# A graph network's gathered blocks: one visit of six rounds in place of two of three

## The chip, the cores and the metric

The kernel runs on one core of a Trainium2 chip. The metric is the device time in microseconds of one execution; the median of the runs is quoted. The engines are named as the profile names them: PE is TensorE, DVE is VectorE, ACT is ScalarE, POOL is GpSimd, SP is the queue of SyncE. PEld is TensorE's loading of weights.

## The reference

A graph with 6250 nodes, 256 features each, and 100000 edges sorted by destination. Four layers; each adds to every node the sum of its sources' features and then runs a small dense network over the nodes.

```python
h = jnp.maximum(_layernorm(x, axis=-1), 0.0)
def agg(h):
    return jax.ops.segment_sum(h[src], dst, num_segments=N)
for l in range(NL - 1):                       # three layers, 256 -> 256 -> 256 -> 256
    h = x + agg(x)
    h = jax.nn.relu(h @ W1s[l] + b1s[l])
    h = jax.nn.relu(h @ W2s[l] + b2s[l])
    x = h @ W3s[l] + b3s[l]
h = x + agg(x)                                # the last one, 256 -> 256 -> 64 -> 256
h = jax.nn.relu(h @ cW1 + cb1)
h = jax.nn.relu(h @ cW2 + cb2)
out = x_in + (h @ cW3 + cb3)
```

## The kernel before

The nodes are cut into 49 blocks of 128. The sum over the edges is done in two ways, side by side.

Most blocks are summed by a **product**: a matrix of edge counts, 128 destinations by all nodes, is built once as bytes (layer 0 builds it while it uses it, lines 1030 to 1093), kept in DRAM and cast to fp32r when it is used (line 1565). TensorE multiplies it with the features XY, which are held in SBUF as a high and a low half. In layer 0 the products go block by block (line 1588), in layers 1 to 3 by panels of four blocks (line 1665), with single blocks (line 1588) in between. A panel has 49 steps of four matmuls with 512 columns; a step is the unit in which the program is laid out.

The other blocks are **gathered**: 23 in layer 0, 20 in layers 1 and 2, 19 in layer 3. The edges of a gathered block are held in T = 17 tiles of 128 edges. For each tile GpSimd issues an indirect DMA (line 1382) that fetches the 128 source rows from the layer's table in DRAM into one of the buffers `rows`: 24 of them in layer 0, 25 in layers 1 to 3. TensorE then adds the rows up with one-hot matrices as the weights. Because the edges are sorted, a tile can only touch a neighbourhood of the block: the block's 128 destinations are four groups of Q = 32, and tile c + 4m serves group m in round c. There are six rounds, c = -1, 0, 1, 2, 3, 4; a round is four matmuls (three for c = -1) with 32 weight columns each, which fill the four column groups of the array, and in fp32 each matmul is two instructions of the profile. So a block has 23 matmuls, 46 instructions, that add up in one bank of PSUM, `sums`.

The six rounds are done in two **visits**, ROUNDS = ((3, 1, -1), (0, 4, 2)). A visit (`add`, line 1408) is put between two steps of the products. The first needs the 8 odd tiles, the second the 9 even ones. The one-hots of a visit come from one VectorE instruction (line 1402), which compares a row of column numbers with the table `rel`; it is issued right after the visit before, and has two buffers. After a block's second visit its own features are added (lines 1439 and 1448), two blocks at a time are transposed (line 1479), and the dense network follows for four blocks at a time (lines 1233 and 1290; in the last layer 1225 and 1245).

The order of all work is fixed while the program is written out: each engine runs its instructions in that order. A planner keeps an estimated clock, which `passed` moves on with every matmul (constants in line 1508; a visit counts as VISIT = 1.7 us). When a layer's table is complete, `begin` fixes when its first visit is due, LEAD = 21 us of this clock later, and spreads the others evenly up to TAIL = 10 us before the layer's estimated end; `pace` is the time per row. `flow` sends the row requests at the same pace, LEAD ahead, and ties each to the last matmul written so far (`after`), so that GpSimd can't issue it earlier. `meets` says whether a visit is due; eight steps before the end of a layer all visits that are left are due. Steps of the dense network wait in a queue and are taken at a visit where one falls into their window, or else at the window's end (`step`). In layer 0 the first 8 requests are sent at once, before the build of the counts starts (line 1703).

Of the kernel before, what the change touches and what calls it, by code (L numbers as in the profile page):

```python
# [8 lines left out]
F32 = mybir.dt.float32  # L9
# [387 lines left out]
def sorted_edges(  # L397
# [58 lines left out]
    CUTS = ((3, 5), (7, 9), (11, 13), (0, T))  # L456
    ROUNDS = ((3, 1, -1), (0, 4, 2))
    CH = 7
# [38 lines left out]
    idx = const.tile([P, left[NQ]], I32, name="idx")  # L497
    rel = const.tile([P, left[NQ] // T, len(ROUNDS), 3, P // Q], BF16, name="rel")
    colf = const.tile([P, P], F32, name="colf")
# [117 lines left out]
    def look(pool):  # L617
# [214 lines left out]
        for t, o in ((fd, rel), (fs, idx)):  # L832
            ps = ps_m.tile([P, W], F32, name="ps")
            for q, (_, n) in enumerate(gone):
                nc.tensor.transpose(ps[:, left[q]:left[q + 1]], t[:n * T, q, :],
                                    ident[:n * T, :n * T])
            if o is rel:
                v = ps[:, :left[NQ]].rearrange("p (b k) -> p b k", k=T)
                for i, rounds in enumerate(ROUNDS):
                    for c in rounds:  # L840
                        g = 1 if c < 0 else 0
                        nc.vector.tensor_scalar(o[:, :, i, (c - min(rounds)) // 2, g:],
                                                v[:, :, c + 4 * g:c + 13:4], -1.0, None, op0=OP.add)
            else:
                nc.vector.tensor_copy(o, ps[:, :left[NQ]])
# [118 lines left out]
    with tc.manual_schedule():  # L964
# [370 lines left out]
        class Gathered:  # L1335
            def __init__(self, l):
# [10 lines left out]
                self.n = len(self.visits)  # L1347
                self.rows, self.us = {}, []

# [16 lines left out]
            def begin(self):  # L1366
                self.first = clock[0] + LEAD
                self.end = begun[self.l] + work_of(self.l) - TAIL
                self.pace = (self.end - self.first) / (self.upto[-1] - self.upto[1])
# [27 lines left out]

            def one_hots(self, v):
                g, rounds = self.visits[v]
                shape = [P, len(rounds), P // Q, Q]  # L1400
                self.hot = work.tile(shape, F32, name="hot", bufs=2)
                nc.vector.tensor_tensor(
                    self.hot,
                    colf.rearrange("p (m q) -> p m q", q=Q)[:, None, :, :].to_broadcast(shape),
                    rel[:, self.blocks[g][3] // T, v % len(ROUNDS), :, :, None].to_broadcast(shape),
                    OP.is_equal)

            def add(self):
# [3 lines left out]
                self.sums = sums  # L1412
                if v == 0:
                    self.one_hots(0)
                end = rounds == ROUNDS[-1]
                for c in rounds:
                    for m in range(P // Q):
                        if c + 4 * m >= 0:
                            nc.tensor.matmul(  # L1419
                                self.sums[m * Q:(m + 1) * Q, :C],  # L1420
                                self.hot[:, (c - min(rounds)) // 2, m, :], self.rows[g, c + 4 * m],
                                start=(c == ROUNDS[0][0]), stop=(c == ROUNDS[-1][-1]))
                passed(VISIT)
                self.done += 1
                if self.done < self.n:
                    self.one_hots(self.done)
                if end:
# [78 lines left out]
        sums = ps_g.tile([P, W], F32, name="sums")  # L1506
        LEAD, TAIL = 21.0, 10.0
        COLS, FULL32, TURN, VISIT, BUILD, BURST = 0.457e-3, 1.68e-3, 0.4, 1.7, 0.2, 0.3
        clock = [0.0]
# [183 lines left out]
        with tc.tile_pool(name="hots", bufs=1) as hots, tc.tile_pool(  # L1693
# [8 lines left out]
            layers[0].begin()  # L1702
            layers[0].send(layers[0].upto[1])
            beside = build(hots, ats, ps_b)
# [84 lines left out]
```

## Time and profile before

| | |
|---|---|
| median of 3 runs | 2130.42 us (2127.44 to 2132.5) |
| the profiled execution | 2135.8 us, its span 2134.0 us |
| TensorE, mean granted clock | 0.988 |
| PE / PEld busy | 96% / 70% of the span |
| DVE / ACT / POOL busy | 44% / 41% / 68% |
| chain that ended last, by engine | PE 88%, DVE 5%, DMA 4%, the rest 3% |
| row requests by layer, first to last | 126.6 to 674.2, 719.2 to 1163.3, 1205.7 to 1647.6, 1686.8 to 2105.0 |

A group of the profile has the line, the engine, the operation, what is written from what, the count, the busy time in us, the mean in ns of one, and then the idle time of the engine ahead of these instructions with what ended it. Rows of the timeline have start, duration, engine, line and a count of merged instructions, and in brackets the idle time ahead and what ended it. The chain is followed back from the last instruction, at each step to what released it; "issue" is time in which an engine waited for nothing that the profile shows. The view of stretches gives each engine's busy time and its instructions (x) between two times, then the granted clock, the busy share of the DMA engines and GB/s. A view of one line or tile gives the shortest, the median and the longest duration in ns, and the first and the last start.

### The profile page before, as it was taken

The numbers are of one execution on the slowest core, as the hardware profiler recorded it, in microseconds if no ns is written. First come the engines' busy times: TensorE is split into PE (matmuls) and PEld (weight loads), VectorE is DVE, ScalarE is ACT, GpSimd is POOL, SyncE is SP. The second block draws the span as 40 slices with busy tenths as digits, with TensorE's granted clock in tenths as the row PEclk, the third lists the DMA queues.
The fourth block names the chain that finished last, engine by engine and source line by source line (L and its number), as shares of the span: only waits on it lengthen the run. The fifth ranks groups of instructions, "written<-read, shape, count | busy, mean of one in ns | idle before, by whom it ended". The sixth has DMA issues, their size and how long they took to land.

```text
span 2134.0 us, 33393 instructions
## 1 busy us (share of the span) xinstructions
PE 2057.4 (96%) x12076; PEld 1487.8 (70%) x12076; DVE 937.7 (44%) x2192; ACT 864.3 (41%) x1775; POOL 1445.4 (68%) x1470
## 2 busy tenths in 40 slices
PE   4979999999999999999999999999999999999997
PEld 3756766667667777777776777777776777777675
DVE  7877867667673422222233322222233433333332
ACT  4856655556556522323232433222333432223231
POOL 2727777777774477777776377777776277777773
PEclk9979999999999999999999999999999999999999
DMA  5524545545455655455455554555456555556553
GB/s 157 176 98 139 162 142 153 158 140 164 150 158 152 213 163 155 153 181 164 142 186 167 173 160 148 173 165 169 146 168 195 170 172 181 184 180 194 183 160 119
DMA packets 184901, 347.61 MB, mean 163 GB/s; under 512 B 32446, under 2 KB 118496, under 8 KB 184726
## 3 DMA queue, kind: packets, MB, share of 16 engines
q0 software_dynamic: 68960, 185.41, 29.7%
q1 hardware_dynamic: 113838, 158.12, 22.3%
q8 instruction: 97, 1.59, 0.3%
q10 hardware_dynamic: 1928, 1.85, 0.3%
q14 instruction: 78, 0.64, 0.1%
HBM read 287.98 MB, written 57.26 MB: 162 GB/s over the span
## 4 chain that ended last, share of the span: by engine, by line
PE 88%; DVE 5%; DMA 4%; issue 1%; ACT 1%; POOL 1%; SPq 0%; DVEq 0%; POOLq 0%; ACTq 0%
PE agg L1665 43%; PE agg L1588 16%; PE sums L1419 11%; PE ps L1233 6%; PE ps L1290 6%; PE bp L1076 4%; DMA rows<-table,idx 3%; PE ps L1479 1%; POOL rows L1382 1%; DVE junk L695 1%; PE bp L920 1%; DVE hi L1035 1%; DVE at L1086 1%; PE ps L1245 0%; DMA table<-zs 0%
## 5 line engine op out<-in xcount | busy, mean ns | idle before, releaser
L1382 POOL DMA_INDIRECT rows<-table,idx x1394 | 1387.7, 995 | 611.4 <-issue 220.6
L1665 PE MATMUL agg<-a,XY 128*128 128x512 f32 x4116 | 982.8, 395 | 1.9 <-DVE clT L1600 1.9
L1665 PEld LDWEIGHTS agg<-a,XY 128*128 128x128 f32 x4116 | 764.6, 188 | 209.5 <-issue 45.8
L1565 ACT CAST a<-at 128x512 fp32r<-128x512 uint8 (+1 forms) x542 | 326.9, 616 | 576.9 <-PE agg L1665 543.9
L1565 DVE CAST a<-at 128x512 fp32r<-128x512 uint8 x543 | 242.7, 448 | 552.8 <-PE agg L1665 469.3
L1588 PE MATMUL agg<-XY,a 128*128 128x512 f32 x1470 | 404.9, 409 | 1.3 <-DVE un L1600 0.7
L1588 PEld LDWEIGHTS agg<-XY,a 128*128 128x128 f32 x1470 | 258.9, 189 | 53.7 <-issue 8.7
L1419 PE MATMUL sums<-rows,hot 128*32 128x256 f32 x3772 | 256.0, 385 | 16.2 <-DMA rows<-table,idx 15.0
L1419 PEld LDWEIGHTS sums<-rows,hot 128*32 128x32 f32 x3772 | 112.6, 109 | 142.6 <-issue 53.6
L1549 ACT CAST a<-at 128x512 fp32r<-128x512 uint8 (+2 forms) x362 | 196.7, 574 | 6.5 <-PE agg L1588 6.5
L1084 ACT CAST at<-bp 128x392 uint8<-128x392 f32 x240 | 116.6, 487 | 203.7 <-PE bp L1076 191.0
L1086 DVE CAST at<-bp 128x392 uint8<-128x392 f32 x240 | 135.1, 563 | 138.2 <-PE bp L1076 138.2
L1448 DVE TENSOR_TENSOR u<-u,sums 128x256 f32<-128x256 f32 x82 | 34.3, 419 | 241.8 <-PE agg L1665 226.9
L1076 PE MATMUL bp<-hi,lo 128*128 128x196 bf16 x960 | 127.5, 255 | 11.0 <-DVE hi L1035 10.7
L1290 PE MATMUL ps<-w,h 128*128 128x256 f32 x588 | 133.9, 379 | 1.4 <-ACT h L1236 0.9
L1233 PE MATMUL ps<-h,w 128*128 128x512 f32 (+3 forms) x332 | 133.9, 545 | 0.6 <-DVE zz L1298 0.6
L1035 DVE TENSOR_TENSOR hi<-cols,pairs 128x784 bf16<-128x784 bf16 x240 | 134.3, 560 | 0.0
L1076 PEld LDWEIGHTS <-lo 128*128 128x128 bf16 x960 | 70.6, 99 | 81.9 <-DVE hi L1035 27.8
L1290 PEld LDWEIGHTS ps<-w,h 128*128 128x128 f32 x588 | 111.1, 190 | 18.7 <-ACT h L1236 1.8
L1483 ACT ACTIVATE h<-ps,bias 128x256 f32<-128x256 f32 (+1 forms) x116 | 47.2, 464 | 154.9 <-PE ps L1479 154.9
L1298 DVE TENSOR_TENSOR zz<-ps,w 128x512 f32<-128x512 f32 (+1 forms) x75 | 50.1, 678 | 117.0 <-PE ps L1290 117.0
L1035 DVE TENSOR_TENSOR lo<-lanes,pairs 128x512 bf16<-128x512 bf16 x240 | 100.3, 418 | 1.3 <-ACT pairs L1030 1.3
(171 smaller groups left out, 989.7 us busy)
## 6 DMA issues: line engine op xcount, KB each, us to landing
at<-mat SPq DMA_DIRECT2D x151, 448.0 KB
mat<-at SPq DMA_DIRECT2D x30, 784.0 KB
rows<-table,idx POOLq DMA_INDIRECT x1394
table<-zz SPq DMA_DIRECT2D x72, 256.0 KB
back<-table SPq DMA_DIRECT2D x99, 128.0 KB
xs<-in_x_dram SPq DMA_DIRECT2D x8, 768.0 KB
table<-zs SPq DMA_DIRECT2D x24, 256.0 KB
out_dram<-zz SPq DMA_DIRECT2D x24, 256.0 KB
```

The source lines that it names most:

```text
L1035: nc.vector.tensor_tensor(o.rearrange("p q (n t) -> p q n t", t=2), values.rearrange("p (n t) -> p n t", t=2)[:, None, :, :].to_broadcast( ...
L1076: mm = nc.tensor.matmul(bp[:, m * HW:(m + 1) * HW], lo[:, q + m, :], hi[:, q + m, :], start=True, stop=True)
L1084: nc.scalar.copy(o, v)
L1086: nc.vector.tensor_copy(o, v)
L1233: mm = nc.tensor.matmul(ps[:mp, :w], weights[l][0][:, c, i * P:i * P + mp], h1[:, c, :w], start=(c == 0), stop=(c == KC - 1))
L1290: mm = nc.tensor.matmul(o, h2[0][:, c, nodes], w3[:, c, :], start=(c == 0), stop=(c == KC - 1))
L1382: got = nc.gpsimd.indirect_dma_start(out=t, out_offset=None, in_=tables[self.l][:, :], in_offset=bass.IndirectOffsetOnAxis(ap=idx[:, o:o + ...
L1419: nc.tensor.matmul(self.sums[m * Q:(m + 1) * Q, :C], self.hot[:, (c - min(rounds)) // 2, m, :], self.rows[g, c + 4 * m], start=(c == ROUND ...
L1549: nc.scalar.copy(a[:, i * m * P:(i + 1) * m * P].rearrange("p (j d) -> p j d", j=m), counts[b][:, j:j + m, :])
L1565: cast(o, at[:, :, d:d + m * P])
L1588: mm = nc.tensor.matmul(agg, a[:, d:d + P], XY[:, j, :], start=(j == 0), stop=(j == NT - 1))
L1665: mm = nc.tensor.matmul(agg[c][:, :w], XY[:, j, o:o + P], a[:, :w], start=(j == 0 and half == 0), stop=(j == NT - 1 and half == 1))
```

## The change

All six rounds of a block are done in one visit. Its one-hots are one instruction of twice the size (768 columns of fp32) into one buffer, made four steps after the visit before, and for a layer's first block when the layer begins. A visit now needs all 17 tiles of its block. LEAD goes from 21 to 32 us and VISIT from 1.7 to 3.0 us (it counted twice per block before). Layer 0's first 8 requests stay 8, now by number. `rel` has the same size in another order.

```diff
-    ROUNDS = ((3, 1, -1), (0, 4, 2))
+    ROUNDS = ((3, 1, -1, 0, 4, 2),)
...
-    rel = const.tile([P, left[NQ] // T, len(ROUNDS), 3, P // Q], BF16, name="rel")
+    rel = const.tile([P, left[NQ] // T, len(ROUNDS), len(ROUNDS[0]), P // Q], BF16, name="rel")
...
-                        nc.vector.tensor_scalar(o[:, :, i, (c - min(rounds)) // 2, g:],
+                        nc.vector.tensor_scalar(o[:, :, i, c - min(rounds), g:],
...
-                self.rows, self.us = {}, []
+                self.rows, self.us, self.hots = {}, [], -1
...
             def begin(self):
                 self.first = clock[0] + LEAD
+                self.one_hots(0)
...
             def one_hots(self, v):
+                if self.hots >= v:
+                    return
+                self.hots = v
                 g, rounds = self.visits[v]
                 shape = [P, len(rounds), P // Q, Q]
-                self.hot = work.tile(shape, F32, name="hot", bufs=2)
+                self.hot = work.tile(shape, F32, name="hot")
...
-                if v == 0:
-                    self.one_hots(0)
+                self.one_hots(v)
...
-                                self.hot[:, (c - min(rounds)) // 2, m, :], self.rows[g, c + 4 * m],
+                                self.hot[:, c - min(rounds), m, :], self.rows[g, c + 4 * m],
...
                 if self.done < self.n:
-                    self.one_hots(self.done)
+                    later(4, lambda v=self.done: self.one_hots(v))
...
-        LEAD, TAIL = 21.0, 10.0
-        COLS, FULL32, TURN, VISIT, BUILD, BURST = 0.457e-3, 1.68e-3, 0.4, 1.7, 0.2, 0.3
+        LEAD, TAIL = 32.0, 10.0
+        COLS, FULL32, TURN, VISIT, BUILD, BURST = 0.457e-3, 1.68e-3, 0.4, 3.0, 0.2, 0.3
...
-            layers[0].send(layers[0].upto[1])
+            layers[0].send(8)
```

## The prediction

> **What bounds the kernel now.** I read the page first (busy shares, then the costliest groups), then the busy time of each engine by layer, then the GpSimd queue by layer, then the chain of work at the ends of layers.
>
> ```profile
> span 2134.0 us, 33393 instructions
> ...
> PE 2057.4 (96%) x12076; PEld 1487.8 (70%) x12076; DVE 937.7 (44%) x2192; ACT 864.3 (41%) x1775; POOL 1445.4 (68%) x1470
> ...
> L1382 POOL DMA_INDIRECT rows<-table,idx x1394 | 1387.7, 995 | 611.4 <-issue 220.6
> ```
>
> By the shares TensorE bounds everything and GpSimd (POOL) has a third of its time free. The second view, one stretch per layer from its first row request to its last, has the same TensorE story: 443.21 busy of 446, 444.00 of 444.
>
> ```profile
> core 0: us, PE busy (x) PEld busy (x) DVE busy (x) ACT busy (x) POOL busy (x), PEclk, DMA share, GB/s
> 126.00:676.00 550.00, 536.78 (x3571) 371.11 (x3572) 386.71 (x893) 326.97 (x748) 394.66 (x391) 0.98 0.50 152
> 719.00:1165.00 446.00, 443.21 (x2525) 324.18 (x2523) 132.61 (x305) 140.76 (x258) 337.66 (x340) 1.00 0.56 173
> 1205.00:1649.00 444.00, 444.00 (x2534) 325.48 (x2532) 132.31 (x297) 138.86 (x251) 334.26 (x340) 1.00 0.56 172
> 1686.00:2107.00 421.00, 414.03 (x2464) 304.19 (x2462) 136.23 (x301) 126.77 (x229) 321.07 (x323) 1.00 0.59 184
> ```
>
> But GpSimd's free time is not free. The next rows are its groups in the same four stretches; the number that matters is the idle time before the requests.
>
> ```profile
> L1382 POOL DMA_INDIRECT rows<-table,idx x391 | 394.7, 1009 | 173.6 <-issue 63.9 <-PE agg L1588 45.5 <-PE bp L1076 34.8
> ...
> L1382 POOL DMA_INDIRECT rows<-table,idx x340 | 337.7, 993 | 151.5 <-issue 56.1 <-DMA back<-table 44.1 <-PE agg L1665 39.9
> ...
> L1382 POOL DMA_INDIRECT rows<-table,idx x340 | 334.3, 983 | 150.0 <-issue 53.7 <-PE agg L1665 44.7 <-DMA w<-in_L_gnn_W2s_dram 41.4
> ...
> L1382 POOL DMA_INDIRECT rows<-table,idx x323 | 321.1, 994 | 136.3 <-issue 46.9 <-DMA clT<-in_L_gnn_cW_dram 38.2 <-PE agg L1665 37.8
> ...
> 1162.09 0.95 POOL rows L1382
> 1163.04 0.30 issue
> 1163.34 3.99 DMA rows<-table,idx
> 1167.38 1.92 PE sums L1419 x10
> ```
>
> Between two requests that follow at once lies 0.30 us. Leave out each layer's one long wait for its table (44.1, 41.4, 38.2) and count 0.30 per request: layer 1 has 151.5 - 44.1 - 340 x 0.30 = 5.4 us of true idleness on GpSimd, layer 2 has 150.0 - 41.4 - 102 = 6.6, layer 3 has 136.3 - 38.2 - 96.9 = 1.2. Only layer 0 has room: 173.6 - 117.3 = 56. So in layers 1 to 3 the row requests run back to back from the moment the table is complete to the last row, at 0.99 + 0.30 = 1.29 us each, and the layer's end waits for the last of them: the chain above goes request, 3.99 us of flight, sums. TensorE is full and the request queue is full as well. A gain on TensorE in layers 1 to 3 is capped by what the queue can still give.
>
> **The change, part by part.** (1) Two visits of three rounds become one of six. A visit works the array as 128x32 tiles between full-width products; its surroundings cost time that no round needs.
>
> ```profile
> 1061.11 3.46 PE ps L1290 x16
> 1064.56 1.43 PE sums L1419 x24
> 1065.99 4.76 PE agg L1665 x20
> 1070.76 1.43 PE sums L1419 x22
> 1072.19 11.12 PE agg L1665 x48
> 1083.31 1.43 PE sums L1419 x24
> ...
> 1201.88 21.80 PE agg L1665 x96
> ...
> 161.71 1.50 PE L1419 MATMUL sums<-rows,hot 128*32 128x256 f32 x22 [1.11 <-DVE hot L1402]
> ...
> 209.44 1.50 PE L1419 MATMUL sums<-rows,hot 128*32 128x256 f32 x22
> 210.87 0.51 PE L1076 MATMUL bp<-hi,lo 128*128 128x196 bf16 x4
> ```
>
> A pass of 256 fp32 columns takes 3.46 / 16 = 0.216 us; a round is two passes (four column groups side by side), so three rounds are 1.30, and 1.43 is spent: 0.13 over. An undisturbed product runs at 21.80 / 96 = 0.227; 48 between two visits should take 10.90 and take 11.12: 0.22 more, the way in and out of a visit. A visit's surroundings thus cost about 0.35 us, and the merge removes one per block. At 17 rows a block the requests above are 23, 20, 20 and 19 blocks. Layers 1 to 3: 59 x 0.35 = 20.7 us of TensorE time (7.0, 7.0, 6.7). In layer 0 what follows is often a build (L1076) whose slow-down I cannot read off; bounds 0.13 and 0.35, taken 0.25: 5.8 us. All layers: 26.5.
>
> (2) The first one-hot is made when the layer begins, not in the first visit: the 1.11 us wait at 161.71 goes. What is late next there is nothing, the rows then have 32 planned us.
>
> (3) What of this reaches the end. Layer 0 is bound by TensorE (56 us of idle requests): all of it counts, less the last visit. At the end of a layer the planner flushes what is left eight steps before the end, and the last row then in flight now holds up a visit of six rounds, not three. Its first four rounds need rows 0, 1, 3, ... up to 15, so they can run while row 16 flies; I charge 1 us. Layer 0: -5.8 - 1.1 + 1 = -5.9. Layer 1: TensorE offers 7.0, less about 2 because with the new lead one or two requests more (1.29 each) are still unsent at the flush; GpSimd can give at most 5.4, and never all: -3.5. Layer 2: 7.0 against 6.6: -4.5. Layer 3: GpSimd has 1.2 to give, the earlier finish only lengthens TensorE's waits for rows: 0, and +0.5 for the longer last visit.
>
> (4) One-hots: one instruction of 768 columns for two of 384, in one buffer, four steps after the visit.
>
> ```profile
> L1402 DVE TENSOR_TENSOR hot<-colf,rel x164: 537/551/607, 161.1 to 2092.2; 128x384 f32<-128x384 f32 x164
> ...
> L1439 DVE TENSOR_TENSOR u<-XY x82: 410/418/427, 174.3 to 2101.3; 128x256 f32<-128x256 f32 x82
> ...
> 2037.93 0.56 DVE L1402 TENSOR_TENSOR hot<-colf,rel 128x384 f32<-128x384 f32 x1
> 2038.40 0.42 DVE L1439 TENSOR_TENSOR u<-XY 128x256 f32<-128x256 f32 x1
> ...
> 2036.73 0.95 POOL L1382 DMA_INDIRECT rows<-table,idx  x1 [0.30 <-PE agg L1665]
> 2037.98 1.33 POOL L1382 DMA_INDIRECT rows<-table,idx  x1 [0.30 <-issue]
> ...
> L1382 POOL DMA_INDIRECT rows<-table,idx x323: 947/953/1582, 1686.8 to 2105.0; - x162
> ```
>
> From 384 and 256 columns the slope is (0.551 - 0.418) / 128 = 1.04 ns a column, so 768 take 0.551 + 0.400 = 0.95: 82 x (1.10 - 0.95) = 12 us less on VectorE, which is a third busy in layers 1 to 3, so nothing by itself. The single buffer makes the one-hot wait for the visit before. Ahead of it in VectorE's order stands the add at L1448, three steps after the visit, which waits for the same sums and a product behind them; so the one-hot finds its buffer free, and the casts behind it wait for no more than before. Its cover is the distance to the next visit, some 446 / 20 = 22 us; were it gone, each visit would wait 0.95.
>
> But the request at 2037.98 met one-hot and add: 1.33 instead of 0.95. The requests of layers 1 to 3 average 0.993, 0.983 and 0.994 where the median, in the last row, is 0.953: 13.6 + 10.2 + 13.2 = 37 us in all, in the very queue that is full. If what a request loses grows with the square of an uninterrupted VectorE run (chance to meet it, times what is left of it), two of 0.55 against one of 0.95 is 0.61 to 0.90, at worst half of 37 more: +18. Yet in every second visit one-hot and add stand together today (0.98) and will stand apart: 1.26 to 1.08, -5. Between -5 and +18 I take 0, nearest to the second count, which is what the rows show.
>
> (5) The lead. It was 21 planned us for a first visit of 8 rows, now 32 for one of 17. At a planned pace near 1.35 us (an estimate; the rows come every 446 / 340 = 1.31) that is 15.6 - 8 + 1 = 8.6 rows ahead of need, and 23.7 - 17 + 1 = 7.7 now: the same. New is that 17 + 8 = 25 fills the 25 buffers (24 in layer 0, 17 + 7). A request beyond them waits on GpSimd, with all later ones behind it, until the visit is through. The count of requests issued by the start of a visit shows how far ahead the queue runs today:
>
> ```profile
> 719.00:782.75 63.75, 49.41 (x47) 1.00 0.63 202
> 719.00:1019.76 300.76, 229.45 (x230) 1.00 0.56 173
> ```
>
> The visit at 782.75 needed row 42, that at 1019.76 row 221: 5 and 9 rows ahead. With a cap of 8 the late visits cost GpSimd a row's time, but the queue is only held where it had run ahead, and 5 rows x 1.29 = 6.5 us still cover the 3.99 us flight. I take 0; the far bound is the third rival.
>
> (6) Table `rel`, its six writes, the first 8 requests: the same work in another order, 0.
>
> Sum: -5.9 - 3.5 - 4.5 + 0.5 = -13.4 us. The profiled execution took 2135.8 us for its span of 2134.0, 0.25% above the median of 2130.42; it would become 2122.4, and the median **2117.0**. Bounds of the parts: layer 0 from -3 to -9, layers 1 and 2 from -4 to -12, layer 3 from -1 to +1: 2114 to 2124 for this case.
>
> **The rivals.** *The whole TensorE gain arrives.* If the queue is not the bound, because the requests keep their pace with TensorE and only look back to back, 26.5 + 1.1 come off: 2103. For it: TensorE 99% busy in layers 1 and 2. Against it: 1.2 us of idle requests in layer 3, and layer ends that wait for rows.
>
> *The longer one-hot slows the requests.* By (4) between 9 (the one-hots behind half of the 37 us) and 18 us come back: about 2130, no change. The Trainium skill, "SBUF — State Buffer", section "Who interferes with whom", has a tensor_tensor with both inputs in SBUF contend with GpSimd's reads, the second to come blocked for the whole of the first. The trace agrees in the 1.33 us request; by that rule alone the longer instruction is the worse.
>
> *Steps move behind the last rows.* Steps of the dense layers (3.46 us at 1061.11) prefer to run at a visit and otherwise wait for their deadline; with half the visits more of them slip. One that slips past the flush in each of layers 0 to 2 costs 3 x 3.5 = 10: 2127. Against it: the last steps of a layer are hurried anyway.
>
> *The full buffers stop the queue: slower.* Each late visit leaves GpSimd idle with 25 rows out, and the queue has only 5.4 and 6.6 us of slack to catch up. Layer 3 runs behind and never fills its buffers, so it is the 40 blocks of layers 1 and 2: from 13.4 / 40 = 0.33 us lost per block on, the gain is eaten; at half a request, 0.65 us, it is 40 x 0.65 - 13.4 = +12.6, 2143; at 0.5 us, 2137. For it: 9 rows ahead at 1019.76. Against it: a held queue was ahead, and TensorE only feels it once the lead falls under the flight.
>
> **How the numbers follow.** Forecast 0.50, whole gain 0.08, one-hot 0.12, steps 0.12, buffers 0.18. A measurement of this kernel tells about 0.2%, 4.3 us, from no change: the limits are 2126.2 and 2134.7. Faster: 0.48 of the forecast, the whole gain, 0.03 of the one-hot and 0.06 of the steps: 0.65. Slower: 0.15 of the buffers, 0.04 of the one-hot and 0.01 of the steps: 0.20. The rest, 0.15, is the same. The range leaves out the whole gain and the far end of the buffers: 2108 to 2138.
>
> **What would show it.** Right: visits of 46 matmuls in 2.7 to 2.8 us; first to last row request of layer 3 still 418 us (1686.8 to 2105.0 now), of layers 1 and 2 some 4 us shorter, layer 0 5 to 6; more TensorE waiting on rows in layer 3. Wrong: a mean request above 1.00 us (one-hot), requests that wait on the sums for more than a few us in all (buffers), a 3.5 us step between the last visit and the next layer's first request that is not there today, or layer 3 shorter by 6 us (whole gain).

## The result: slower by a quarter of a per cent

The merged kernel takes 2137.67 us, median of 9 runs (2134.25 to 2141.0); the kernel before, run beside it, 2130.74 (9 runs, 2127.44 to 2135.63). The ratio on record is 1.0025, with an interval of 1.0014 to 1.0037; the two medians are 6.9 us apart, 0.33%. The forecast was 2117.0, faster by 0.6%: the direction was wrong, and the time lies at the upper end of the range.

The profile after comes from an execution of 2136.97 us. That of the kernel before, which the prediction reads, took 2135.8 us, 5 us over its median, so a second profile of the same kernel is used for the comparison: 2130.95 us, at the median. First the page of the merged kernel:

```profile
span 2134.9 us, 33269 instructions
PE 2038.4 (95%) x12076; PEld 1499.3 (70%) x12076; DVE 930.6 (44%) x2110; ACT 859.5 (40%) x1775; POOL 1448.2 (68%) x1470
L1383 POOL DMA_INDIRECT rows<-table,idx x1394 | 1390.9, 998 | 605.3 <-issue 219.1
L1422 PE MATMUL sums<-rows,hot 128*32 128x256 f32 x3772 | 249.5, 391 | 29.7 <-DMA rows<-table,idx 29.6
L1422 PEld LDWEIGHTS sums<-rows,hot 128*32 128x32 f32 x3772 | 124.2, 111 | 147.0 <-DMA rows<-table,idx 43.5
```

The busy times and the same two rows of the visits on the page of the kernel before (its second profile):

```profile
PE 2054.6 (96%) x12076; PEld 1486.3 (70%) x12076; DVE 937.6 (44%) x2192; ACT 864.2 (41%) x1775; POOL 1445.9 (68%) x1470
L1419 PE MATMUL sums<-rows,hot 128*32 128x256 f32 x3772 | 254.4, 385 | 15.1 <-DMA rows<-table,idx 14.0
L1419 PEld LDWEIGHTS sums<-rows,hot 128*32 128x32 f32 x3772 | 112.2, 109 | 140.7 <-issue 51.9
```

TensorE is busy for less time: 2038.4 us instead of 2054.6. But it waits longer for rows: 29.6 us at the visits instead of 14.0. The requests' mean (998 ns against 996 before) has hardly moved.

Where the time went is read by layer. The next two answers give the busy time of each engine from the start of one layer's products to the start of the next layer's. The kernel before:

```profile
139.60:693.30 553.70, 545.82 (x3611) 378.80 (x3611) 375.95 (x870) 331.43 (x761) 386.47 (x383) 1.00 0.49 151
693.30:1181.60 488.30, 482.87 (x2696) 354.65 (x2697) 147.78 (x339) 158.07 (x300) 337.45 (x340) 0.99 0.53 166
1181.60:1664.60 483.00, 480.34 (x2692) 352.38 (x2691) 147.21 (x331) 154.92 (x286) 334.38 (x340) 1.00 0.53 167
1664.60:2129.20 464.60, 447.40 (x2613) 327.50 (x2611) 153.02 (x340) 138.04 (x254) 322.72 (x323) 0.99 0.56 174
```

The merged kernel:

```profile
140.80:696.80 556.00, 542.39 (x3610) 383.37 (x3610) 372.74 (x846) 329.30 (x761) 383.86 (x383) 0.99 0.50 151
696.80:1182.10 485.30, 475.85 (x2696) 357.68 (x2697) 145.73 (x319) 157.52 (x300) 339.95 (x340) 0.99 0.54 167
1182.10:1664.60 482.50, 477.40 (x2691) 356.51 (x2690) 145.17 (x312) 153.28 (x286) 335.82 (x340) 0.99 0.54 167
1664.60:2134.90 470.30, 444.68 (x2615) 328.94 (x2613) 152.32 (x321) 137.58 (x255) 322.98 (x323) 0.98 0.56 172
```

The second column is the length, the third TensorE's busy time; their difference is TensorE's idle time. The clock is the third figure from the right.

| layer | length, us | TensorE busy | TensorE idle | predicted length |
|---|---|---|---|---|
| 0 | +2.3 | -3.4 | 7.9 to 13.6 | -5.9 |
| 1 | -3.0 | -7.0 | 5.4 to 9.4 | -3.5 |
| 2 | -0.5 | -2.9 | 2.7 to 5.1 | -4.5 |
| 3 | +5.7 | -2.7 | 17.2 to 25.6 | +0.5 |

Busy time fell by 16.1 us, idle time grew by 20.6. (The first profile of the kernel before has 553.1, 489.8, 484.3 and 464.1 us for the four layers: two executions of the same kernel differ by up to 1.5 us in a layer.) The granted clock is lower too: 0.982 to 0.987 in the nine executions of the merged kernel, 0.987 to 0.991 in ten of the kernel before.

**Layer 0: a lump on VectorE.** The time that the count build's matmuls (L1076) wait for VectorE's casts (L1035) over layer 0, as total, number of times and longest; before, then merged:

```profile
PE bp L1076 <- DVE hi L1035: 3.4, 10, 0.6
```

```profile
PE bp L1076 <- DVE hi L1035: 8.7, 19, 1.7
```

Its longest piece in the timeline of the merged kernel, VectorE first, then TensorE:

```profile
321.68 0.41 DVE L1451 TENSOR_TENSOR u<-u,sums 128x256 f32<-128x256 f32 x1
322.01 0.95 DVE L1406 TENSOR_TENSOR hot<-colf,rel 128x768 f32<-128x768 f32 x1
322.88 0.42 DVE L1035 TENSOR_TENSOR lo<-lanes,pairs 128x512 bf16<-128x512 bf16 x1
323.21 0.56 DVE L1035 TENSOR_TENSOR hi<-cols,pairs 128x784 bf16<-128x784 bf16 x1
```

```profile
323.83 0.51 PE L1076 MATMUL bp<-hi,lo 128*128 128x196 bf16 x4 [1.71 <-DVE hi L1035]
```

The add of the sums (0.41 us) and the 0.95 us one-hot stand together in front of the two casts for which the next build matmuls wait 1.71 us. The add of the sums ends just ahead of the one-hot in 36 of the 82 blocks of the merged kernel, 9 in each layer.

**The ends of layers: the 16th row.** The last visits of layer 2 in TensorE's timeline, before:

```profile
1640.60 1.50 PE L1419 MATMUL sums<-rows,hot 128*32 128x256 f32 x22
...
1644.10 1.06 PE L1419 MATMUL sums<-rows,hot 128*32 128x256 f32 x14
1647.20 1.05 PE L1419 MATMUL sums<-rows,hot 128*32 128x256 f32 x10 [2.04 <-DMA rows<-table,idx]
```

The last visit of layer 1, the last two of layer 2, and the last of layer 3, merged:

```profile
1158.98 1.06 PE L1422 MATMUL sums<-rows,hot 128*32 128x256 f32 x2 [4.36 <-DMA rows<-table,idx]
1164.20 4.25 PE L1422 MATMUL sums<-rows,hot 128*32 128x256 f32 x40 [4.15 <-DMA rows<-table,idx]
...
1628.22 2.80 PE L1422 MATMUL sums<-rows,hot 128*32 128x256 f32 x46
...
1637.05 0.62 PE L1422 MATMUL sums<-rows,hot 128*32 128x256 f32 x4
1638.49 0.62 PE L1422 MATMUL sums<-rows,hot 128*32 128x256 f32 x2 [0.82 <-DMA rows<-table,idx]
1642.90 5.33 PE L1422 MATMUL sums<-rows,hot 128*32 128x256 f32 x40 [3.80 <-DMA rows<-table,idx]
...
2103.80 5.33 PE L1422 MATMUL sums<-rows,hot 128*32 128x256 f32 x40 [3.35 <-DMA rows<-table,idx]
```

A block's rows are requested in the order of their numbers. The first round (c = 3) of the merged visit uses tiles 3, 7, 11 and 15, and tile 15 is the 16th of 17 requests: 6 matmuls run, and 40 wait for the row before the last. In the kernel before, only the odd tiles stand in the first visit, and only 10 matmuls wait for the last row. And the 40 take 5.33 us, where the whole visit of 46 before it takes 2.80. Busy time and clock in short stretches around the last visit of layer 3 say why:

```profile
2095.00:2100.00 5.00, 5.00 (x29) 3.69 (x30) 1.44 (x3) 2.91 (x7) 3.78 (x5) 1.00 0.37 108
2100.00:2103.80 3.80, 0.46 (x6) 0.00 (x0) 0.00 (x0) 0.00 (x0) 2.62 (x3) 0.82 0.36 104
2103.80:2106.50 2.70, 2.70 (x28) 1.32 (x32) 0.00 (x0) 0.00 (x0) 0.00 (x0) 0.50 0.18 49
2106.50:2109.10 2.60, 2.60 (x21) 0.85 (x13) 0.00 (x0) 0.00 (x0) 0.00 (x0) 0.50 0.00 0
2109.10:2112.00 2.90, 2.28 (x10) 1.63 (x10) 1.62 (x4) 0.00 (x0) 0.00 (x0) 0.97 0.00 0
```

After the wait of 3.35 us TensorE's clock is 0.50 for the whole 5.3 us of the visit. The length of the wait alone does not decide this. Here are waits of the kernel before (first and second profile) and of the merged kernel with half of its requests (an experiment below):

```profile
1652.49 1.05 PE L1419 MATMUL sums<-rows,hot 128*32 128x256 f32 x10 [3.28 <-DMA rows<-table,idx]
...
1907.46 1.05 PE L1419 MATMUL sums<-rows,hot 128*32 128x256 f32 x10 [2.53 <-DMA rows<-table,idx]
1908.50:1911.50 3.00, 3.00 (x8) 2.42 (x8) 0.93 (x2) 0.00 (x0) 2.13 (x3) 0.50 0.35 102
...
1156.94 4.46 PE L1426 MATMUL sums<-rows,hot 128*32 128x256 f32 x40 [2.13 <-DMA rows<-table,idx]
```

The wait of 3.28 us was followed by a clock of 1.00, those of 2.53 and 2.13 by a clock of 0.50 for some 3 us; the 40 matmuls behind a wait of 2.11 us in the merged kernel took 2.78 us, full speed. The Trainium skill, "TensorE: Matmul & The Clock Gate", section "Part 1: The HAM clock gate", says that an idle window of about 3.4 us halves the clock until about as long a busy one has passed. The waits of 3.35 to 4.36 us agree with it, those of 2.13 and 2.53 us do not, and the measurement decides: here waits between 2.1 and 3.3 us went either way.

Summed in slices of 1 us as (1 - clock) x TensorE's busy time, the half clock costs 2.1, 2.0, 0.0 and 2.8 us in layers 0 to 3 before, and 2.9, 2.0, 2.8 and 4.4 merged: an estimated 5.3 us more. Added to the 16.1 us by which the busy time fell, TensorE's saving at full clock is about 21 us, where the prediction had 26.5.

### The profile page after: what moved, and what is told of

It reads as the page before. It is cut to its first block, busy times and chain, and to the rows that moved or that the text cites. A ratio compares the mean times of both kernels' runs of the same rounds, so it can differ in the third digit from the quotient of the medians.

```text
span 2134.9 us, 33269 instructions
## 1 busy us (share of the span) xinstructions
PE 2038.4 (95%) x12076; PEld 1499.3 (70%) x12076; DVE 930.6 (44%) x2110; ACT 859.5 (40%) x1775; POOL 1448.2 (68%) x1470
## 3 DMA queue, kind: packets, MB, share of 16 engines
q1 hardware_dynamic: 113838, 158.12, 22.6%
## 4 chain that ended last, share of the span: by engine, by line
PE 85%; DVE 6%; DMA 4%; ACT 2%; issue 2%; POOL 1%; SPq 0%; DVEq 0%; ACTq 0%; POOLq 0%
PE agg L1668 42%; PE agg L1591 13%; PE sums L1422 11%; PE ps L1290 6%; PE ps L1233 6%; PE bp L1076 3%; DMA rows<-table,idx 3%; DVE hi L1035 1%; DVE at L1086 1%; PE ps L1482 1%; PE bp L920 1%; DVE lo L1035 1%; POOL rows L1383 1%; PE ps L586 1%; DVE hot L1406 1%
## 5 line engine op out<-in xcount | busy, mean ns | idle before, releaser
L1422 PE MATMUL sums<-rows,hot 128*32 128x256 f32 x3772 | 249.5, 391 | 29.7 <-DMA rows<-table,idx 29.6
L1422 PEld LDWEIGHTS sums<-rows,hot 128*32 128x32 f32 x3772 | 124.2, 111 | 147.0 <-DMA rows<-table,idx 43.5
L1076 PE MATMUL bp<-hi,lo 128*128 128x196 bf16 x960 | 127.9, 256 | 17.2 <-DVE hi L1035 16.5
L1035 DVE TENSOR_TENSOR hi<-cols,pairs 128x784 bf16<-128x784 bf16 x240 | 134.3, 559 | 0.0
L1076 PEld LDWEIGHTS <-lo 128*128 128x128 bf16 x960 | 72.0, 99 | 87.0 <-DVE hi L1035 37.6
L1233 PEld LDWEIGHTS ps<-h,w 128*128 128x128 f32 (+1 forms) x332 | 60.9, 189 | 56.0 <-issue 47.1
```

The lines of the kernel that those rows point to most:

```text
L1035: nc.vector.tensor_tensor(o.rearrange("p q (n t) -> p q n t", t=2), values.rearrange("p (n t) -> p n t", t=2)[:, None, :, :].to_broadcast( ...
L1076: mm = nc.tensor.matmul(bp[:, m * HW:(m + 1) * HW], lo[:, q + m, :], hi[:, q + m, :], start=True, stop=True)
L1233: mm = nc.tensor.matmul(ps[:mp, :w], weights[l][0][:, c, i * P:i * P + mp], h1[:, c, :w], start=(c == 0), stop=(c == KC - 1))
L1422: nc.tensor.matmul(self.sums[m * Q:(m + 1) * Q, :C], self.hot[:, c - min(rounds), m, :], self.rows[g, c + 4 * m], start=(c == ROUNDS[0][0] ...
```

## The experiments

**How well the same kernel repeats.** The kernel before, unchanged; it also gave the second profile used above.

> The kernel before, unchanged, run as if it were a change: it tells how far two equal kernels come apart and gives a second profile by layer. Expected on every theory: a ratio of 1.000 within 0.2%, and a profiled execution nearer the median than the first one (2135.8 against 2130.7), row requests of layers 1 to 3 again 444, 442 and 418 us from first to last.

Measured: 2131.45 us, ratio 0.9996 (0.9981 to 1.0011), as expected.

**Half of the requests left out, before and merged.**

```diff
                     g, k = self.order[self.sent]
+                    if self.sent % T % 2:
+                        self.rows[g, k] = self.rows[self.order[self.sent - 1]]
+                        self.sent += 1
+                        continue
```

> The kernel before with 9 of a block's 17 row requests: every second tile of a block uses the rows of the tile before it, so 738 requests are left and the output is not the reference's. Theory 'the request queue caps layers 1 to 3': the queue is half empty, so TensorE's waits for rows go (about 7 us at the end of layer 1, 4 of layer 2, 12 in layer 3) and the time falls by 15 to 25 us. Rival 'the queue only looks full': within 5 us of before.

> The changed kernel with the same 738 requests. Theory 'the queue caps layers 1 to 3': with the cap gone the merged visits bring their 0.35 us a block there, so it is 17 to 21 us faster than the kernel before with half the requests, all of it in layers 1 to 3. Rival 'the merge saves nothing on TensorE, or VectorE takes it back in every layer': within 6 us of it.

Measured: before 2109.15, ratio 0.9899 (0.9868 to 0.9929); merged 2094.78, ratio 0.9823 (0.9791 to 0.9855). The visits' rows on the two pages, before and merged:

```profile
L1423 PE MATMUL sums<-rows,hot 128*32 128x256 f32 x3772 | 246.8, 383 | 1.8 <-DVE hot L1406 1.1
```

```profile
L1426 PE MATMUL sums<-rows,hot 128*32 128x256 f32 x3772 | 232.3, 383 | 3.1 <-DMA rows<-table,idx 3.1
```

So the request queue is a bound of the kernel before (22 us; by the two profiles 7.1, 2.6 and 13.3 in layers 1 to 3), as the prediction read it from GpSimd's gaps. And with rows in time, the merge is worth 14.4 us: with the full queue it costs 7. That is less than the 17 to 21 expected. By layer the merge gives +1.1, -1.9, -5.4 and -6.2 us there, while TensorE's busy time falls by 19.0. The saving on TensorE is real; a good part of what eats it depends on the rows.

**The later one-hots left out.** In the merged kernel only a layer's first block makes its one-hot (4 instead of 82); in the kernel before likewise its first visit.

```diff
 merged:
-                if self.hots >= v:
+                if self.hots >= 0:
                     return
 before:
             def one_hots(self, v):
+                if v:
+                    return
```

> The changed kernel with one one-hot for a whole layer in place of one a block, which leaves out 78 of the 82 instructions at 0.95 us; the output is not the reference's. Theory 'the long one-hot stands in front of VectorE's one-hots for the build in layer 0': layer 0 gets 6 to 8 us shorter, TensorE's wait for the build falls back from 8.7 to about 3 us. Theory 'it also holds up requests': their mean in layers 1 to 3 falls from 0.998 by 0.02 or more, 7 us a layer. Together 15 to 25 us below the changed kernel. Rival 'the one-hot has no part in it': within 4 us of the changed kernel.

> The kernel before with one one-hot for a whole layer (156 to 160 of 164 instructions of 0.55 us are left out; the output is not the reference's). Theory 'layer 0 is bound by VectorE's chain already': layer 0 falls by 3 us or more from 553.6, though TensorE's work is the same, and the gain of the changed kernel without one-hots (549.3) over this one in layer 0 is under 2 us. Theory 'layer 0 is bound by TensorE and only the long one-hot broke that': layer 0 stays at 552 to 554 here, and the changed kernel without one-hots is 4 us shorter. In layers 1 to 3 the mean request falls by 0.01 to 0.02, and the total is 8 to 15 us below before.

Measured: merged 2115.08, ratio 0.9925 (0.9901 to 0.9949); before 2126.38, ratio 0.9983 (0.9968 to 0.9999). The merged kernel gives up 22.6 us with its 78 one-hots, the kernel before 4.4 with its 160: the one-hots as merged cost 18 us more, and without them the merge would gain 11.3, near the forecast's 13.4. The 22.6 is what was expected; the 4.4 is less than the 8 to 15 expected for the kernel before. In layer 0 the build's wait for the casts is back at the old value without the one-hots (merged):

```profile
PE bp L1076 <- DVE hi L1035: 3.9, 11, 0.8
```

and layer 0 of the merged kernel lasts 549.3 instead of 556.0 us; that of the kernel before 553.3 without, 553.7 with its one-hots. Without one-hots the merge gives layer 0 -4.0, close to the -5.9 of the prediction. In layers 1 to 3 it shows in the queue. The requests of these layers in the merged kernel, with and then without its one-hots:

```profile
L1383 POOL DMA_INDIRECT rows<-table,idx x340 | 339.9, 1000 | 145.3 <-PE agg L1668 77.0 <-issue 54.5 <-DMA rows<-table,idx 4.0
...
L1383 POOL DMA_INDIRECT rows<-table,idx x340 | 335.8, 988 | 143.0 <-PE agg L1668 73.9 <-issue 56.1 <-PE ps L1290 3.7
...
L1383 POOL DMA_INDIRECT rows<-table,idx x323 | 323.0, 1000 | 137.9 <-issue 43.9 <-DMA clT<-in_L_gnn_cW_dram 39.8 <-PE agg L1668 37.2
```

```profile
L1383 POOL DMA_INDIRECT rows<-table,idx x340 | 332.9, 979 | 148.1 <-PE agg L1668 76.3 <-issue 61.5 <-PE ps L1233 3.0
...
L1383 POOL DMA_INDIRECT rows<-table,idx x340 | 331.2, 974 | 146.0 <-PE agg L1668 76.9 <-issue 59.4 <-PE ps L1290 2.4
...
L1383 POOL DMA_INDIRECT rows<-table,idx x323 | 317.0, 982 | 136.9 <-issue 46.3 <-DMA clT<-in_L_gnn_cW_dram 38.8 <-PE agg L1668 33.5
```

The requests take 7.0, 4.6 and 6.0 us less. In the kernel before, the same edit takes 5.1, 3.0 and 5.9 us off them (means of 992, 983 and 999 ns to 977, 975 and 981), so the merged one-hots cost the requests only some 4 us more. But they count for more: in the kernel before the edit shortened layers 1 and 2 by only 0.5 and 0.2 us, in the merged kernel by 4.2 and 2.9; layer 3 fell in both, by 6.2 and 7.9. TensorE is busy for 482.58 of 487.8 us and 480.33 of 482.8 in layers 1 and 2 of the kernel before without one-hots; that it is TensorE that keeps the faster requests from counting there is argued, not shown. TensorE's waits for rows in the merged kernel fell from 29.6 to 19.2 us.

**The one-hot in two halves of 384 columns,** four and eight steps after the visit, in the same buffer:

```diff
-                    later(4, lambda v=self.done: self.one_hots(v))
+                    later(4, lambda v=self.done: self.one_hots(v, 1))
+                    later(8, lambda v=self.done: self.one_hots(v))
```

> The one-hots in two instructions of 384 columns, four and eight steps after the visit, once more, because the chip of the last four runs took 11% longer for the kernel before, with long gaps on GpSimd and TensorE in which neither waited for work. Expected of a chip like the first: theory 'the length of one uninterrupted VectorE run stalls the build': layer 0 3 to 5 us shorter than in the changed kernel (556), the total 4 to 10 us below 2137. Rival 'the place of the one-hot, in the middle of the build's steps, is what costs': layer 0 as in the changed kernel or longer.

Measured: 2130.45, ratio 0.9998 (0.9985 to 1.001): level with the kernel before, and below the merge's 1.0025, some 6 us, as expected. (This run, the next one, the halves with the short window and the extra product in the kernel before fell on another chip of the same speed, where the kernel before takes 2129.83 and the merged kernel wasn't run; so the ratios are compared.) Layer 0 lasts 552.7 us, 3.3 less than merged; the requests of layers 1 to 3 average 0.990, 0.987 and 0.990 us. The length of the instruction is thus a part of its price, not all: the waits for casts in layer 0 are 6.6 us, those for rows 23.6.

**The one-hot one step after the visit instead of four,** ahead of the add of the sums:

```diff
-                    later(4, lambda v=self.done: self.one_hots(v))
+                    later(1, lambda v=self.done: self.one_hots(v))
```

> The changed kernel with the one-hot one step after the visit in place of four: the same instruction of 768 columns, placed where VectorE has to wait for the visit itself, which still reads the single buffer. Theory 'the place costs': layer 0 3 to 6 us shorter than the changed kernel's 556. Theory 'the length costs': layer 0 the same within 2 us, or longer by up to 5, since VectorE now also stands still until the visit of 2.7 us is through.

Measured: 2132.54, ratio 1.0015 (1.0005 to 1.0025). The interval overlaps the merge's (1.0014 to 1.0037), so a gain in the whole time isn't shown. No one-hot stands behind an add any more, and layer 0's wait for casts is 7.0 us with a longest of 0.8, where it was 8.7 and 1.7; but layer 0 lasts 554.2 us, 1.8 less than merged. That is within the 2 us of 'the length costs', not the 3 to 6 of 'the place costs'.

**A shorter window for the dense steps** (3 instead of 6), in both kernels, and with the halves:

```diff
-        FAR, SPAN = 7, 6
+        FAR, SPAN = 7, 3
```

> The kernel before with SPAN at 3. Theory 'SPAN repairs what the merge did to the steps': with two visits a block a step meets a visit in time anyway, so the time stays within 3 us of before, the tail after the last request near 28 us as before. Rival 'a shorter window is better for any kernel': 5 to 10 us below before, as much as on the changed kernel.

> The changed kernel with SPAN at 3 and its one-hots as they are. Theory 'the slipped steps cost the tail': from the last request to the end 28 to 30 us in place of 32.6, the total 3 to 8 us below the changed kernel, 2130 to 2135. Rival 'the gain of the combined kernel came from the split one-hots with some luck': 2136 to 2139.

> Split one-hots and SPAN at 3 together, on the changed kernel: the two losses that the trace of the changed kernel shows beside the full queue. If both theories hold (layer 0 -4, the tail after the last request from 32.6 us to about 28) the time is 7 to 12 us below the changed kernel: 2125 to 2130, at or just under the kernel before. If only the tail holds: 2132 to 2135. If neither: 2137.

Measured: before 2121.71, ratio 0.9956 (0.9943 to 0.9969); merged 2128.71, ratio 0.9988 (0.9972 to 1.0004); merged with halves 2122.28, ratio 0.9956 (0.9942 to 0.997). The window is worth 9 us to either kernel, as the rival 'a shorter window is better for any kernel' had it, so steps that slip are not what makes the merge slower: it stays 7.0 us behind with the short window, though its tail from the last request to the end fell from 32.6 to 25.9 us (before: 27.8 to 25.1). With the halves its ratio is level with that of the kernel before, as it was with the long window. The waits for rows at the visits with the window of 3, before and then merged:

```profile
PE sums L1419 <- DMA rows<-table,idx: 6.4, 6, 2.7
```

```profile
PE sums L1422 <- DMA rows<-table,idx: 22.4, 11, 4.5
```

The kernel before now waits 6.4 us in pieces of at most 2.7, the merged one 22.4 in pieces of up to 4.5. On these chips the kernel before with the window of 3 and the merged one with halves and window share the lowest ratio of those that compute the reference, 0.9956; no merged version was shown to beat the kernel before with the same window.

**One more block as a product instead of gathered** in layers 1 and 2, in the kernel before (34 requests fewer, more TensorE work):

```diff
-        solos = [[], [19], [19], [18, 19]]
+        solos = [[], [18, 19], [18, 19], [18, 19]]
-        order = [[]] + [[0, 1, 2, 19, 3, 4, 5, 6]] * 2 + [[0, 1, 18, 2, 3, 19, 4, 5, 6]]
+        order = [[]] + [[0, 1, 18, 2, 3, 19, 4, 5, 6]] * 3
```

> The kernel before with block 18 as a product in layers 1 and 2, once more on another chip. Theory 'TensorE and the queue are both full within some us': 2 to 8 us above before. Rival 'the queue alone is the bound of layers 1 and 2': 20 us or more below.

Measured: 2140.0, ratio 1.0049 (1.0031 to 1.0066), 10 us above, somewhat more than the 2 to 8 expected. Layers 1 and 2 get longer by 7.6 and 4.5 us while GpSimd has 31 and 33 us to spare: TensorE is full in the kernel before, as the prediction had it.

**A chip on which the kernel before is 11% slower.** Four runs fell on a chip where the kernel before took 2365.62 us (2361.32 to 2374.11), and three more on one where it took 2391.99. They are compared there, not with the runs above. The halves, the window, and the block as a product in both kernels:

> The changed kernel with each block's one-hots in two instructions of 384 columns, four and eight steps after the visit, into the same tile. Theory 'it is the length of one uninterrupted VectorE run that stalls the build in layer 0 and the requests after it': layer 0 gets 3 to 5 us shorter, the mean request of layers 1 to 3 falls by about 0.005 (2 us a layer): 6 to 10 us below the changed kernel, so about the kernel before or a little under. Rival 'it is their total time': the total grows by 82 x 0.15 = 12 us of VectorE, no gain, 0 to 3 us above the changed kernel.

> The changed kernel with SPAN at 3 in place of 6: a dense step or a transposition waits three steps less for a visit to share. At the end of the last layer that puts one dense step (L1225) back ahead of the last visit and the last block's own (L1233) ahead of the last panel's end, where the kernel before has them. Theory 'the steps that slipped behind the last rows cost the tail': from the last row request to the end falls from 32.6 us to 28 to 30, the total by 3 to 5 us. Rival 'the tail is noise of one profile': no change of the tail, total within 2 us.

> The kernel before with block 18 as a product instead of a gathered block in layers 1 and 2 (as it is in layer 3 already): 17 requests less, 22 us of the queue, and some 8 us more on TensorE in each of the two layers. Theory 'TensorE and the queue are both full, within 4 to 7 us': the queue's gain is capped by TensorE, layer 1 gets 0 to 3 us longer, layer 2 3 to 5: 3 to 8 us above before. Rival 'the queue alone is the bound': 20 us or more below before.

> The changed kernel with the same block 18 as a product in layers 1 and 2. Theory 'the queue caps what the merge saves in layers 1 and 2': TensorE waits 11.7 and 8.1 us for rows at the ends of these layers in the changed kernel, so here the 8 us of the product fit into the wait: layer 1 about 3 us shorter, layer 2 as before, 0 to 5 us below the changed kernel; and set against the same edit of the kernel before, the changed one is now equal or better by 0 to 5 us, where it was 7 worse. Rival 'the merge saves TensorE nothing in these layers': again 5 to 8 us worse than the other kernel with the same edit.

Measured: merged with halves 2407.84, ratio 1.0176 (1.0159 to 1.0193); merged with the window 2388.0, 1.0091 (1.0061 to 1.0121); before with the block as a product 2319.45, 0.9802 (0.9783 to 0.9821); merged with it 2366.79, 1.0007 (0.9986 to 1.0028). The merged kernel itself wasn't run on this chip, so the expectations set against it stay open. For the block as a product in the kernel before the rival fits: taking 34 requests off the queue gained 46 us, where it lost 10 on the other chip, so the bounds are others here. With the same block the merged kernel is 47 us behind, more than either expectation had.

The last three runs asked whether the order of the requests is the rest of the loss. The rows are requested in the order in which the rounds use them, so that the last row holds up only the last pair of matmuls:

```diff
-                return sorted({c + 4 * m for c in rounds for m in range(P // Q) if c + 4 * m >= 0})
+                return list(dict.fromkeys(c + 4 * m for c in rounds for m in range(P // Q) if c + 4 * m >= 0))
```

> The merged kernel, with each block's 17 rows requested in the order in which its rounds use them (3, 7, 11, 15, 1, 5, ... 2, 6, 10, 14) instead of the order of their numbers. In the merged kernel the first round needs tile 15, which is the 16th of 17 requests: 40 of a visit's 46 matmuls stand behind the row before the last, and where rows are late TensorE waits once for 3.35 to 3.80 us and then works at a granted clock of 0.50 for some 5 us. Theory (the wait on the 16th row, and the clock that falls behind it): the long waits go, the clock's mean comes back from 0.985 to about 0.989, each layer's end is some 2 to 3 us earlier, 8 to 12 us in all: 2126 to 2130, like the kernel before or a little faster. Rival (it is the one-hots alone, and a full queue sets the end whatever the order): the last row comes when it came, no more than 3 us: 2134 to 2138.

> The merged kernel with requests in the order of use, the one-hot in two instructions of 384 columns four and eight steps after the visit, and the dense steps in the window of 3 steps. With the split and the window it took 2122.3. Theory of the 16th row: 8 to 12 us less, 2110 to 2115, below the kernel before with the window of 3 (2121.7). Rival: 2120 to 2123.

> The kernel before with requests in the order of use and the window of 3 steps; control for the merged one with the same two edits. It took 2121.7 with the window alone; its visits of 8 and 9 rows wait for at most 2.5 us now. Theory: 2119 to 2122. Rival (the order of use is worth the same to any kernel): 2110 to 2114.

Measured, against 2391.99: merged with the order 2424.89, ratio 1.0138 (1.0111 to 1.0166); with order, halves and window 2403.18, 1.0047 (1.0031 to 1.0063); before with order and window 2371.48, 0.9924 (0.99 to 0.9948). They fell on a chip of the slow kind, on which the merged kernel without the edit wasn't run, so what the order is worth in time stays open, and with it the expectations. With order and window the merged kernel, halves and all, is 32 us behind the kernel before there. What TensorE's visits wait for is to be seen, in the merged kernel with the window alone, the merged one with the order alone, and the kernel before with order and window:

```profile
PE sums L1422 <- issue: 55.3, 106, 1.7
PE sums L1422 <- DMA rows<-table,idx: 7.4, 3, 4.0
```

```profile
PE sums L1422 <- issue: 64.9, 115, 1.7
PE sums L1422 <- DMA rows<-table,idx: 4.1, 7, 0.9
```

```profile
PE sums L1419 <- issue: 16.7, 30, 1.5
PE sums L1419 <- DMA rows<-table,idx: 3.4, 3, 1.8
```

With the order of use the longest wait for a row is 0.9 us (1.3 with halves and window); the three merged kernels without it had 4.0 to 4.8 on the other slow chip. So the long wait on the 16th row is gone in these traces, though the two sets come from different chips. The largest wait of a merged kernel's visits on these chips is "issue", in which no releaser shows: 52 to 66 us in the five merged kernels, 17 in the visits of the kernel before. The kernel before has such gaps elsewhere, 47.5 us in front of its panels in the last run, so they do not by themselves explain how far the merged kernels are behind. On the first two chips TensorE's visits have none of it in either kernel.

## Why the prediction was wrong

**What bounds the kernel: right.** Queue and TensorE are both near their limit in layers 1 to 3: half of the requests gave 22 us, and the extra product cost 10. After the merge GpSimd's idle time beyond 0.30 us a request is 1.2 to 1.5 us in each of these layers, as the cap would have it.

**(1), TensorE's saving: right in kind, somewhat large.** About 21 us at full clock (an estimate from the traces) against 26.5. The visits of 46 matmuls take 2.80 us, as it said.

**(2): right in part.** In layer 0 of the merged kernel no visit waits for a one-hot any more. What the 1.1 us is worth in the whole time nothing tells apart.

**(4), the one-hots at 0: the step that failed most.** It counted 12 us less on VectorE, "nothing by itself", with VectorE a third busy in layers 1 to 3; its own row of layer 0 has VectorE busy for 386.71 of 550 us. It did name the casts behind the one-hot, and wrote that they "wait for no more than before", because the one-hot would find its buffer free. It asked whether the one-hot is held up, not how long it holds up what stands behind it. In layer 0 that is the build: the waits for casts went from 3.4 to 8.7 us. With (3)'s "layer 0 is bound by TensorE" taken as if VectorE were free there, the prediction gave -5.9, and it became +2.3; without the later one-hots the merge has -4.0 there. In the count of VectorE's runs it also had the one-hot and the add "stand apart", for -5 of its 37 us; the add of the block's own features does, but the add of the sums now stands right ahead of the one-hot in 36 of 82 blocks. Its end of +18, kept for the range, is the size of the whole difference measured (18), but by luck: the mechanism given for it, slower requests, bears only some 4 us more than before. The rule of the Trainium skill that the prediction cites ("SBUF — State Buffer", "Who interferes with whom") has the right sign: taking the one-hots away shortens the mean request by 8 to 21 ns in the layers of both kernels.

**(3), the last visit at 1 us: under-priced, by how much is less sure.** From the last request to the end of the last visit, layer 2 has 6.8 us (1641.4 to 1648.2) where the second profile of the kernel before has 4.8 (1643.4 to 1648.2) and the first 5.9; layer 3 also has 6.8 (2102.3 to 2109.1) where they have 4.3 (2101.4 to 2105.7) and 5.6. The prediction wrote that the first four rounds "need rows 0, 1, 3, ... up to 15", and did not see that the row 15 in the first round holds back 40 of 46 matmuls, nor that such a wait can halve the clock. Set against the second profile, layer 2's last row came 2.5 us earlier from the start of the layer and 2.0 of it were lost behind it (-0.5 for -4.5). In layer 3 the rest, 2.3 us, lies behind the last visit, where the last dense steps are put in another order; 0.9 in a later last request. Layer 1's -3.0 is near the -3.5, with some luck: its requests took 1.8 us less from first to last, not the 4 of the prediction, layer 2's 3.3. Layer 0's took 5.3 us more, where the prediction had 5 to 6 less.

The losses overlap: faster requests also shorten the waits for rows. How the 18 us divide between VectorE's lump, the requests and the waits is shown by layer, not by cause; and that the order of the rows would have saved the ends of layers is argued from the waits, not shown in time.

**(5), lead and buffers:** in layers 1 to 3 no request waited on the sums for longer than 0.3 us. In layer 0 such waits are 17.6 us (11, the longest 3.8), which is the prediction's own sign for the buffers, in the layer whose queue has time to spare; without the one-hots they are 16.2, and the layer is nearly as short as the merge should make it. Lead and buffers were not tested by themselves.

**The rivals.** The longer one-hot was the right rival, at 0.12, with the wrong victim in layer 0. Its sign, a mean request above 1.00 us, did not show (1.000, 0.988 and 1.000). The whole gain on TensorE did not come; steps that slip are not the difference between the kernels. The full buffers at 0.5 us a block gave 2137, the number measured, but their mechanism in layers 1 and 2, a queue that stands still, did not show there.

## What to carry to other kernels

When small instructions on an engine with time to spare are merged into one, ask what stands behind it in that engine's queue and who waits for that; a third busy in some layers says nothing of the stretch in which the engine feeds the bound. When work is merged on the consumer's side, look up which of its inputs comes last and how much of it stands behind that one; requesting the inputs in the order of use is worth a try, though its worth in time isn't shown here. And count a long wait of TensorE at more than its length where the granted clock falls behind it.

## What the hardware showed that was not expected

- A wait of TensorE for 3.35 or 3.80 us was followed by 40 matmuls at half the clock (5.33 us). So were shorter ones, of 2.53 and 2.13 us, by half the clock for some 3 us, while one of 3.28 us was not; what else decides isn't shown.
- One instruction of 768 columns takes 0.95 us where two of 384 take 1.10, and yet the ratio with the two halves was 0.9998 where it was 1.0025.
- The same kernel took 2131 us on one chip and 2366 on another, and the merge, 0.25% slower on the first, was 2.0% slower on the second than the kernel before with the same edit (2366.79 against 2319.45). The traces of both kernels there show "issue" gaps on TensorE, the merged ones most in front of the small matmuls of the visits; what causes them isn't known.
